# First-layer weighted sums as two float32r matmuls with row sums beside v, in place of weight folding dealt into the first image's attention

## The chip, the core and the metric

The kernel runs on one core of one Trainium2 chip. The core has five engines with a queue each: TensorE (PE, matrix multiplies, with a separate row PEld for the weight loads), VectorE (DVE), ScalarE (ACT), GpSimd (POOL) and SyncE (SP), of which the last only issues DMAs here. Each engine works through its queue in order and waits at an instruction until what it needs is there. The metric is the device time of one execution in microseconds; the number given is the median of three runs.

## The reference

Two attention blocks follow each other on x of shape (8, 512, 32, 32): eight images, 512 channels, T = 1024 positions. The first has eight heads of 64 channels and quantises q, k and v to 8 bits over the whole batch; the second has one head of 512 channels.

```python
# layer 0
h = group_norm(xf, gn_w, gn_b)
qkv = einsum('oc,bct->bot', qkv_w, h) + qkv_b          # then split by head into q, k, v
q, k, v = fake_quant(q), fake_quant(k), fake_quant(v)   # scale from min and max over all images
w = softmax(einsum('bct,bcs->bts', q * scale, k * scale), axis=-1)
a = einsum('bts,bcs->bct', w, v)
x = xf + einsum('oc,bct->bot', proj_w, a) + proj_b
# layer 1
t = group_norm(x)                                       # one head
q, k, v = t @ wq.T + bq, t @ wk.T + bk, t @ wv.T + bv
x = x + (softmax(q @ k.T / sqrt(512)) @ v) @ wp.T + bp
```

Everything is float32. Since the quantisation scales need all images, no score of layer 0 can be computed before q, k and v of all eight images are known.

## The kernel before, in words

Work is cut into tiles of 128 partitions. T is cut into two halves (hf) of 512 and eight blocks (s, t, m) of 128; channels into four blocks (cc, oc, dc) of 128; heads into four pairs (j).

**Phase 1** (lines 213 to 319). For each image, x is loaded and normalised (`norm_steps`, line 99: statistics on VectorE, two tiny matmuls for the group means, then eight writes of h). Eight tiles of q and k (`qkps`, eight matmuls each) and eight tiles of v (`vps`, four each) go through TensorE; VectorE adds the bias, takes max and min, and SP writes the tiles to DRAM. The norm of image b+1 is a generator whose steps are dealt into image b's tiles (line 299). The weight parts of the biases are computed after the first q, k and v tile (`bias`, line 251) by matmuls over all 512 columns. The q, k and v weights are loaded on SP in three column thirds behind the first x (line 240); the second layer's weights go on ScalarE's queue (lines 272 to 274).

**Between.** Lines 323 to 346 reduce the extremes over all partitions and make the scales.

**Phase 2.** `attention` (line 384) runs the first layer's attention as a generator over 512 units (b, j, hf, s), two at a time. `scores` computes one unit's scores for both heads of a pair (`st`, two PSUM buffers of two banks each), ScalarE takes the exp into `pt` (line 405, four buffers), VectorE adds it to a running sum `acc` (lines 408, 410). `weighted` multiplies v by pt for both heads; head 0 writes PSUM partitions 0 to 63 and head 1 partitions 64 to 127 of one bank, so that the two take separate columns of the array. `finish` (line 424) turns `acc` into row sums by two matmuls with ones (`sm`), takes the reciprocal (line 432) and scales (line 434). It is called two units into the next half.

`project` and `layer1` are the work of the second half for one image: `pj` (projection and residual), the second norm, then `g`, `v2ps`, `s2` and `o2`, in chunks of four matmuls that count 4.0 each. The second layer's weights are folded first: wa is a product of wq and wk, wm one of wv and wp (`fold`, line 578).

**The order.** Every matmul made through `mm` (line 92) is tied to the one before it, so TensorE's order is the order of the program text. The loop from line 639 deals attention among the other work: `fold` is interleaved with the first image's attention (`F_FOLD`, line 625), and then for each chunk of image b's other work attention of image b+1 is advanced in proportion (`A_IMAGE / F_IMAGE`). At the steps of the second norm, a negative weight lets attention advance alone by 8, 3 and 3 units of weight (`GN_GAPS`, line 35); the other work then catches up, ahead of its share. On the other engines a scheduler orders instructions by its own estimate.

Of the kernel before, what the change touches and what calls it, by code (L numbers as in the profile page):

```python
# [9 lines left out]
F32 = mybir.dt.float32  # L10
BF = mybir.dt.bfloat16
I32 = mybir.dt.int32
AF = mybir.ActivationFunctionType
# [3 lines left out]
P = 128  # L17
B, C, HH, WW = 8, 512, 32, 32
T = HH * WW
# [27 lines left out]
def attn_pair_kernel(  # L47
# [39 lines left out]
    ident = const.tile([P, P], F32, name="ident")  # L87
    make_identity(nc, ident)

    last_mm = [None]  # L90

    def mm(*args, **kw):
        ins = nc.tensor.matmul(*args, **kw).ins  # L93
        if last_mm[0] is not None:
            tc.add_manual_dep(ins, last_mm[0].name, IN_ORDER, reason="order")
        last_mm[0] = ins


    def norm_steps(src, dst, wcol, bank, nm):
# [32 lines left out]
    def group_norm(src, dst, wcol, bank, nm):  # L132
        for _ in norm_steps(src, dst, wcol, bank, nm):
            pass
# [16 lines left out]
    with ExitStack() as fast:  # L151
# [32 lines left out]
        raw_p = fast.enter_context(tc.tile_pool(name="raw", bufs=3))  # L184
        l1p = fast.enter_context(tc.tile_pool(name="l1p", bufs=1))
        NR0 = B * PAIRS * NH * 2
        chk0 = l1p.tile([NR0, 512], F32, name="chk0")
        chk1 = l1p.tile([B * NH, 512], F32, name="chk1")

        def row_sums(ps, terms):  # L190


            n = len(terms) * CC
            for i, (w, wide) in enumerate(terms):
                for e in range(CC):
                    mm(
                        ps, lhsT=wide[:, e, :], rhs=w[:, e, :],
                        start=(i == 0 and e == 0), stop=(i * CC + e == n - 1),
                    )

        def widen(dst, col):
            for e in range(CC):
                nc.vector.tensor_scalar(
                    dst[:, e, :], ones, vec[:, col + e : col + e + 1], None, ALU.mult
                )

        def by_channel(dst, ps):

            for e in range(CC):
                nc.vector.tensor_mul(ps[:, bass.ts(e, P)], ps[:, bass.ts(e, P)], ident)  # L210
            nc.vector.tensor_reduce(dst, ps.rearrange("p (e n) -> p e n", e=CC), AX.X, ALU.add)

        with tc.tile_pool(name="p1w", bufs=1) as p1w, tc.tile_pool(name="p1", bufs=2) as p1, tc.tile_pool(
# [3 lines left out]

            wn = {}
            for tag, ij in (("h", (NQ1, NK1)), ("v", (NV1, WP1))):
                two = l1p.tile([P, 2, CC, C], F32, tag=tag, name=f"wn_{tag}")  # L220
                for n, i in enumerate(ij):
                    wn[i] = two[:, n]
# [7 lines left out]
            def norm(b):  # L230
                xt = xs.pop(b)
                hs[b] = hn = p1.tile([P, CC, T], F32, tag="h", name=f"h1_{b}")
                return norm_steps(
                    lambda cc, hf: xt[:, cc, bass.ts(hf, 512)],
                    lambda cc, hf: hn[:, cc, bass.ts(hf, 512)],
                    V_GN0W, av_bank, f"a{b}",
                )

            load_x(0)
            for i in range(3):  # L240
                nc.sync.dma_start(
                    wqkv[:, :, bass.ts(i, C)], w_qkv[:, :, bass.ts(i, C)]
                )
            vb = p1w.tile([P, C], F32, name="vb")
            nc.scalar.dma_start(vb, vbias[0:1, :].partition_broadcast(P))
            load_x(1)
            gbb = p1w.tile([P, CC, P], F32, name="gbb")
            widen(gbb, V_GN0B)
            qkb = p1w.tile([P, 2 * PAIRS], F32, name="qkb")

            def bias(i):

                ps = bank(f"bias{i}")
                row_sums(ps, ((wqkv[:, :, bass.ts(i, C)], gbb),))
                if i == 2:
                    nc.vector.tensor_add(vb, vb, ps)  # L256
                    return
                b4 = qkb[:, bass.ts(i, PAIRS)]
                by_channel(b4, ps)
                nc.vector.tensor_add(  # L260
                    b4, b4, vec[:, V_QKB + i * PAIRS : V_QKB + (i + 1) * PAIRS]
                )

            for _ in norm(0):
                pass
            for b in range(B):
                ahead = norm(b + 1) if b + 1 < B else iter(())
                next(ahead, None)
                if b + 2 < B:
                    load_x(b + 2)  # L270
                if b == 1:
                    nc.scalar.dma_start(wp0, w_sq[WP0])
                    for i, w in wn.items():
                        nc.scalar.dma_start(w, w_sq[i])
                hn = hs[b]
                for t in range(2 * PAIRS):
# [3 lines left out]
                    for hf in range(NH):  # L280
                        for cc in range(CC):
                            mm(
# [6 lines left out]
                    if b == 0 and j == 0:  # L289
                        bias(isk)  # L290
# [8 lines left out]
                    if t in (3, 5, 6):  # L299
                        next(ahead, None)  # L300
                for t in range(NT):
                    g = b * NT + t
                    ps = bank(f"vps_{b}_{t}")
                    for cc in range(CC):
                        mm(
# [6 lines left out]
                    if b == 0 and t == 0:  # L312
                        bias(2)
# [5 lines left out]
                del hs[b]  # L319
# [31 lines left out]

        qkp = fast.enter_context(tc.tile_pool(name="qkp", bufs=2))
        ptp = fast.enter_context(tc.tile_pool(name="ptp", bufs=4))
        accp = fast.enter_context(tc.tile_pool(name="accp", bufs=2))
        aop = fast.enter_context(tc.tile_pool(name="aop", bufs=10))
        xp = fast.enter_context(tc.tile_pool(name="xp", bufs=13))
        ptp1 = fast.enter_context(tc.tile_pool(name="ptp1", bufs=10))

# [662 lines left out]
```

## Time and profile before

| | us |
|---|---|
| median of three runs (lowest to highest) | 3114.43 (3112.83 to 3117.67) |
| the profiled execution | 3117.67 |
| its span, first to last instruction | 3115.9 |
| PE busy | 3035.8 |
| VectorE busy | 1688.6 |
| ScalarE busy | 705.0 |
| end of the last v matmul of phase 1 | 703.65 |
| first projection matmul of the first image | 839.35 |
| last projection starts | 2903.86 |

Matmuls of float32 are recorded twice (128x512 f32, x1024 for 512 in the code). Durations of matmuls overlap each other, so the distance between two starts says more than the mean duration. "128*64" in a row of TensorE is the shape of the weights. A row's last part is the idle time of the engine just before the group and what ended it. The mean granted clock was 0.992.

### The profile page before, as it was taken

The numbers are of one execution on the slowest core, as the hardware profiler recorded it, in microseconds if no ns is written. First come the engines' busy times: TensorE is split into PE (matmuls) and PEld (weight loads), VectorE is DVE, ScalarE is ACT, GpSimd is POOL, SyncE is SP. The second block draws the span as 40 slices with busy tenths as digits, with TensorE's granted clock in tenths as the row PEclk, the third lists the DMA queues.
The fourth block names the chain that finished last, engine by engine and source line by source line (L and its number), as shares of the span: only waits on it lengthen the run. The fifth ranks groups of instructions, "written<-read, shape, count | busy, mean of one in ns | idle before, by whom it ended". The sixth has DMA issues, their size and how long they took to land.

```text
span 3115.9 us, 22354 instructions
## 1 busy us (share of the span) xinstructions
PE 3035.8 (97%) x8664; PEld 1162.3 (37%) x8664; DVE 1688.6 (54%) x2024; ACT 705.0 (23%) x793; POOL 20.7 (1%) x28
## 2 busy tenths in 40 slices
PE   6999999999999999999999999999999999999998
PEld 3444444443233333333333333333333333333343
DVE  5555554548955465556455735564555546554322
ACT  0000000005523322333223323232322332233001
POOL 0000000000000000000000000000000000000000
PEclk9999999999999999999999999999999999999999
DMA  5322221113100110101011101100110111000000
GB/s 233 115 102 101 105 104 74 79 77 125 48 21 27 41 48 21 41 28 57 14 59 34 41 20 48 48 21 21 48 48 21 34 34 48 21 21 4 14 10 19
DMA packets 91285, 161.53 MB, mean 52 GB/s; under 512 B 11040, under 2 KB 43808, under 8 KB 90528
## 3 DMA queue, kind: packets, MB, share of 16 engines
q1 hardware_dynamic: 90160, 154.47, 14.2%
q10 hardware_dynamic: 1008, 5.53, 0.4%
q8 instruction: 70, 1.15, 0.2%
q14 instruction: 47, 0.39, 0.0%
HBM read 92.56 MB, written 67.11 MB: 51 GB/s over the span
## 4 chain that ended last, share of the span: by engine, by line
PE 92%; DVE 5%; DMA 1%; issue 1%; ACT 1%; POOL 0%; DVEq 0%; ACTq 0%
PE o L93 15%; PE s L93 15%; PE qkps L93 14%; PE av L93 13%; PE g L93 7%; PE v2ps L93 7%; PE vps L93 7%; PE pj L93 7%; PE st L93 4%; PE sm L93 2%; DVE acc L410 2%; DVE rs L432 2%; DMA wqkv<-in_w_qkv_dram 1%; PE fold L93 1%; PE fold_b L93 0%
## 5 line engine op out<-in xcount | busy, mean ns | idle before, releaser
L405 ACT ACTIVATE pt<-st,esc 128x1024 f32<-128x1024 f32 x512 | 543.1, 1113 | 698.5 <-PE st L93 689.8
L93 PE MATMUL av<-pt,v 128*64 128x512 f32 x2048 | 507.8, 617 | 0.0
L410 DVE TENSOR_TENSOR acc<-acc,pt 128x1024 f32<-128x1024 f32 x384 | 467.1, 1217 | 56.5 <-ACT pt L405 44.0
L93 PE MATMUL o<-p,v 128*128 128x512 f32 x1024 | 466.5, 602 | 3.0 <-ACT rs L564 1.4
L93 PE MATMUL s<-g,h 128*128 128x512 f32 x1024 | 465.2, 601 | 0.0
L93 PE MATMUL qkps<-h,wqkv 128*128 128x512 f32 x1024 | 447.4, 597 | 8.0 <-DMA wqkv<-in_w_qkv_dram 8.0
L93 PEld LDWEIGHTS o<-p,v 128*128 128x128 f32 x1024 | 186.3, 190 | 276.4 <-issue 233.3
L93 PEld LDWEIGHTS s<-g,h 128*128 128x128 f32 x1024 | 187.0, 190 | 269.8 <-issue 230.0
L93 PEld LDWEIGHTS qkps<-h,wqkv 128*128 128x128 f32 x1024 | 194.4, 191 | 247.9 <-issue 246.0
L432 DVE RECIPROCAL rs<-rs 128x512 f32<-128x512 f32 x64 | 214.5, 3351 | 82.0 <-ACT rs L431 81.7
L93 PE MATMUL g<-h,wa 128*128 128x512 f32 x512 | 233.1, 607 | 4.6 <-DVE h L126 4.6
L93 PE MATMUL pj<-ao,wp 128*128 128x512 f32 x512 | 233.0, 602 | 4.1 <-ACT rs L431 4.1
L93 PEld LDWEIGHTS av<-pt,v 128*64 128x64 f32 x2048 | 126.2, 138 | 269.1 <-issue 266.2
L93 PE MATMUL v2ps<-wm,h 128*128 128x512 f32 x512 | 222.9, 594 | 0.0
L93 PE MATMUL vps<-wqkv,h 128*128 128x512 f32 x512 | 221.3, 592 | 0.8 <-DVE vb L256 0.8
L293 DVE TENSOR_SCALAR_CACHE_REDUCE qk<-qkps,qkb 128x1024 f32<-128x1024 f32 x64 | 82.2, 1284 | 217.0 <-PE qkps L93 217.0
L529 DVE COPY v<-v2ps 128x512 f32<-128x512 f32 x64 | 44.2, 691 | 252.7 <-PE v2ps L93 252.7
L541 ACT ACTIVATE p<-s 128x512 f32<-128x512 f32 x128 | 76.5, 598 | 433.6 <-PE s L93 433.6
L545 DVE TENSOR_TENSOR acc<-acc,p 128x512 f32<-128x512 f32 x96 | 66.3, 691 | 196.2 <-ACT p L541 196.2
L93 PE MATMUL st<-q,k 64*128 64x512 bf16 x1024 | 159.0, 386 | 4.9 <-ACT pt L405 4.9
L589 ACT COPY wa<-fold 128x512 f32<-128x512 f32 x4 | 2.3, 586 | 702.0 <-PE fold L93 702.0
L93 PEld LDWEIGHTS g<-h,wa 128*128 128x128 f32 x512 | 95.9, 193 | 142.3 <-issue 111.5
(114 smaller groups left out, 1521.9 us busy)
## 6 DMA issues: line engine op xcount, KB each, us to landing
x<-in_x_dram SPq DMA_DIRECT2D x32, 512.0 KB, 5.7
q_d<-qk SPq DMA_DIRECT2D x32, 512.0 KB, 2.6
raw<-q_d SPq DMA_DIRECT2D x32, 512.0 KB, 3.4
k_d<-qk SPq DMA_DIRECT2D x32, 512.0 KB, 2.6
raw<-k_d SPq DMA_DIRECT2D x32, 512.0 KB, 4.2
v_d<-v SPq DMA_DIRECT2D x64, 256.0 KB, 2.0
raw<-v_d SPq DMA_DIRECT2D x32, 512.0 KB, 4.3
x<-in_x_dram SPq DMA_DIRECT2D x64, 256.0 KB, 2.6
```

The source lines that it names most:

```text
L93: ins = nc.tensor.matmul(*args, **kw).ins
L293: nc.vector.tensor_scalar(qk, ps.rearrange("p a n -> p (a n)"), qkb[:, t : t + 1], None, ALU.add, ALU.max, accum_out=mx[:, g : g + 1],)
L405: nc.scalar.activation(pt, st, AF.Exp, scale=esc)
L410: nc.vector.tensor_add(accs[b, j, hf], accs[b, j, hf], pt)
L432: nc.vector.reciprocal(rs, rs)
L529: nc.vector.tensor_copy(vt[:, t, :], ps)
L541: nc.scalar.activation(pt, ps, AF.Exp, scale=SM1)
L545: nc.vector.tensor_add(acc, acc, pt)
L589: nc.scalar.copy(dst[:, e, :], ps)
```

## The change

Two parts of the kernel are replaced.

1. *Weighted sums.* For each unit, ScalarE computes the exp twice: once into `hi`, of type float32r (a float32 with fewer bits of mantissa[...]), and once in place in PSUM. VectorE subtracts hi from it into `lo`, also float32r. Each head then has a PSUM bank of its own, and `weighted` makes four float32r matmuls with 128 columns: head 0's weights are its 64 columns of v and then 64 columns of ones, head 1's are ones and then v. The other half of each bank so holds the row sums, and `finish` copies both halves out on ScalarE, takes the reciprocal and scales. The running sums `acc` and the `sm` matmuls of the first layer go. hi and lo have three buffers each. `finish` is called right after the last weighted sum of a half.
2. *Weights and order.* The folding is done between phase 1 and attention, nothing is dealt into the first image's attention, and the bias sums are matmuls of one column. The norm of image b+1 is written whole ahead of image b's tiles, and those matmuls are no longer tied in order. The q, k and v weights are loaded on ScalarE's queue by channel block. The check of the row sums moves behind all other work.

```diff
-            row_sums(ps, ((wqkv[:, :, bass.ts(i, C)], gbb),))
+            norm(0)
+            for t in range(2 * PAIRS):
+                for cc in range(CC):
+                    nc.tensor.matmul(
+                        ps[:, t : t + 1], lhsT=wqkv[:, cc, bass.ts(t, P)],
+                        rhs=vec[:, V_GN0B + cc : V_GN0B + cc + 1],
+                        start=(cc == 0), stop=(cc == CC - 1),
+                    )
...
             for b in range(B):
-                ahead = norm(b + 1) if b + 1 < B else iter(())
-                next(ahead, None)
+                if b + 1 < B:
+                    norm(b + 1)
...
-            for i in range(3):
-                nc.sync.dma_start(
-                    wqkv[:, :, bass.ts(i, C)], w_qkv[:, :, bass.ts(i, C)]
-                )
+            for cc in range(CC):
+                nc.scalar.dma_start(wqkv[:, cc, :], w_qkv[:, cc, :])
...
+            for dst, lw, rw in ((wa, NQ1, NK1), (wm, NV1, WP1)):
+                for e in range(CC):
+                    ps = bank(f"fold_{lw}_{e}")
+                    for d in range(CC):
+                        nc.tensor.matmul(
+                            ps, lhsT=wn[lw][:, d, bass.ts(e, P)], rhs=wn[rw][:, d, :],
+                            start=(d == 0), stop=(d == CC - 1),
+                        )
+                    nc.scalar.copy(dst[:, e, :], ps)
...
-        ptp = fast.enter_context(tc.tile_pool(name="ptp", bufs=4))
+        ptp = fast.enter_context(tc.tile_pool(name="ptp", bufs=3))
+        vts = [l1p.tile([P, NT, 3, CH], F32R, name=f"v_{i}") for i in range(2)]
+        for vt in vts:
+            for t in range(NT):
+                nc.scalar.copy(vt[:, t, 1, :], ones[:, 0:CH])
...
-                pt = ptp.tile([P, 2, 512], F32, tag="p", name=f"pt_{nm}_{s}")
-                nc.scalar.activation(pt, st, AF.Exp, scale=esc)
-                if s == 1:
-                    accs[b, j, hf] = accp.tile([P, 2, 512], F32, tag="acc", name=f"acc_{nm}")
-                    nc.vector.tensor_add(accs[b, j, hf], pts[u - 1], pt)
-                elif s > 1:
-                    nc.vector.tensor_add(accs[b, j, hf], accs[b, j, hf], pt)
+                hi = ptp.tile([P, 2, 512], F32R, tag="hi", name=f"hi_{nm}")
+                nc.scalar.activation(hi, st, AF.Exp, scale=esc)
+                nc.scalar.activation(st, st, AF.Exp, scale=esc)
+                lo = ptp.tile([P, 2, 512], F32R, tag="lo", name=f"lo_{nm}")
+                nc.vector.tensor_sub(lo, st, hi)
...
-                for i, r in enumerate(HALF):
-                    mm(
-                        avs[b, j, hf][r, :], lhsT=pairs[b, j][2][:, s, r], rhs=pt[:, i, :],
-                        start=(s == 0), stop=(s == NT - 1),
-                    )
+                for i, bk in enumerate(avs[b, j, hf]):
+                    w = pairs[b, j][2][:, s, i : i + 2, :].rearrange("p i d -> p (i d)")
+                    for n, part in enumerate(parts):
+                        mm(
+                            bk, lhsT=w, rhs=part[:, i, :],
+                            start=(s == 0 and n == 0), stop=(s == NT - 1 and n == 1),
+                        )
...
-                sm = bank(f"sm_{nm}")
-                for i, r in enumerate(HALF):
-                    mm(sm[r, :], lhsT=ones[:, 0:CH], rhs=acc[:, i, :], start=True, stop=True)
-                nc.scalar.copy(rs, sm)
+                for i, bk in enumerate(avs.pop((b, j, hf))):
+                    nc.scalar.copy(rs[HALF[i], :], bk[HALF[1 - i], :])
+                    nc.scalar.copy(aot[HALF[i], :], bk[HALF[i], :])
                 nc.vector.reciprocal(rs, rs)
...
-                if s == 2 and u >= NT:
-                    finish(*units[u - NT][:3])
-                    yield 1.0, b
+                if s == NT - 2:
+                    finish(b, j, hf)
...
-        A_IMAGE = PAIRS * NH * (NT * 1.5 + 1.0)
+        A_IMAGE = PAIRS * NH * NT * 1.25
...
-        folded = 0.0
-        for w in fold():
-            folded += w
-            while pos < (folded - F_FIRST) * A_IMAGE / F_FOLD:
-                advance()
```

## The prediction

> **What bounds the kernel now.** I began with the page's busy times and its chain, then read the groups by shape, and last the timeline of TensorE around the first image's attention and around one second-layer norm.
>
> ```profile
> PE 3035.8 (97%) x8664; PEld 1162.3 (37%) x8664; DVE 1688.6 (54%) x2024; ACT 705.0 (23%) x793; POOL 20.7 (1%) x28
> ...
> PE 92%; DVE 5%; DMA 1%; issue 1%; ACT 1%; POOL 0%; DVEq 0%; ACTq 0%
> ```
>
> TensorE (PE) is busy for 97% and is 92% of the chain; VectorE and ScalarE are followers. The groups:
>
> ```profile
> L405 ACT ACTIVATE pt<-st,esc 128x1024 f32<-128x1024 f32 x512 | 543.1, 1113 | 698.5 <-PE st L93 689.8
> L93 PE MATMUL av<-pt,v 128*64 128x512 f32 x2048 | 507.8, 617 | 0.0
> L93 PE MATMUL st<-q,k 64*128 64x512 bf16 x1024 | 159.0, 386 | 4.9 <-ACT pt L405 4.9
> L432 DVE RECIPROCAL rs<-rs 128x512 f32<-128x512 f32 x64 | 214.5, 3351 | 82.0 <-ACT rs L431 81.7
> L93 PE MATMUL sm<-acc,ones 128*64 128x512 f32 x256 | 69.3, 620 | 0.1
> ```
>
> An f32 matmul leaves two records. The two heads of a pair have 64 columns each and share the array, so av has 2048 records. Durations overlap, so prices come from the distance of starts. The chain's row "676.35 27.48 PE vps L93 x64" gives 429.3 ns a record, 858.6 ns an f32 matmul. The timeline of TensorE, from the end of one projection to the folded-key matmuls (columns: start, us):
>
> ```profile
> 1176.14 0.61 PE L93 MATMUL st<-q,k 64*128 64x512 bf16 x4
> 1176.67 1.94 PE L93 MATMUL av<-pt,v 128*64 128x512 f32 x8
> 1178.54 0.61 PE L93 MATMUL st<-q,k 64*128 64x512 bf16 x4
> ...
> 1193.29 0.58 PE L93 MATMUL gps_b<-gd_b,gavg 128*128 128x4 f32 x2 [3.73 <-DVE gd_b L116]
> ...
> 1198.08 7.13 PE L93 MATMUL g<-h,wa 128*128 128x512 f32 x16 [0.42 <-DVE h L126]
> ```
>
> Two units of attention cost 0.54 us of scores and 1.87 us of weighted sums. Between chunks of other work lies this norm gap of 22 us, filled with attention alone. The same view shows that first-image attention with the folding takes 703.65 to 839.35 (135.7 us); each of seven mixed images takes 294.8 (g at 1198.08 and 1492.85); the last stretch, from 2903.86, takes 212.
>
> **What the Trainium skill says.** "FP8 and Floating Point Precision", TensorE Precision Notes: true FP32 is four passes, reduced precision one. The trace agrees on four: 858.6/4 = 214.7 ns, and the bf16 scores fit one pass a row (0.54 us for two overlapped pairs). No row here is float32r. "TensorE: Matmul & The Clock Gate", LDWEIGHTS: columns/1.2, so 107 ns for 128; the trace has 190 ns per f32 record, hidden under 429. "TensorEngine Tiling (Array Packing)", Key Properties: changing the tiling mode drains; the trace agrees, since scores plus weighted sums are 2.15 us of passes and take 2.41. "ScalarE: Activation LUTs", What ACT_TABLE_LOAD costs: back-to-back ACTIVATEs overlap by 93 ns. Here four exps take 4.14 us, 1.01 each.
>
> **The change, part by part.**
>
> *Weighted sums.* Before, four passes, both heads at once: 4 x 214.7 = 0.86 us a unit. After, two heads x two parts, each on the whole array: again 4 x 214.7 = 0.86. So "one-pass" saves no passes; it saves at most the exposed switching, 1.87 - 1.72 = 0.15 us per two units. The real gain is the row-sum matmul: 64 x about 1.02 us = 65 us.
>
> *ScalarE and VectorE.* Each unit now needs two exps (2.02 us) and a subtraction from PSUM. A 128x1024 TENSOR_TENSOR takes 1.22 (the acc rows); PSUM as a source is no dearer at 512 elements (0.690 in v<-vps against 0.691 in acc<-acc,p). The second exp writes PSUM in place, which no row shows; the skill's ScalarE page calls PSUM the faster destination, so 1.01 is taken as the upper end, and rival (d) is the lower. The subtraction replaces the acc add, so VectorE gains little work. But acc gated nobody; now the score bank is free only after both exps and the subtraction, and there are two banks. Score buffers also hold hi and lo, three of each (before: four pt). In the changed program's order TensorE has scores(u+2), scores(u+3), weighted(u), weighted(u+1); hi(u+3) needs the buffer that weighted(u) frees. Attention alone, after the exps of u+1 end: subtraction 1.3 with its wait, scores 0.3, weighted(u) 0.86, wait 0.2: hi(u+3) starts at 2.66, not 2.02. Two units take 2.02 + 2.66 = 4.68 us, against 2.41 before. Behind hi(u+3) ScalarE queues every later exp and TensorE the next scores.
>
> *Finish.* Four 64x512 copies replace one (0.59 us each, 0.5 pitched: 2.05). They and the reciprocal (3.35) stand ahead of the third subtraction of the next half: 5.4 us instead of 2.0, so +3.4 per eight units. Among chunks this is hidden by 9 us of TensorE work per cycle.
>
> *First image.* Four cycles of 4.68, 3.4, and 0.5 for quantisation make 22.6 us per eight units; x 8 plus 3 to fill = 184.
>
> *Folding moved ahead.* 32 matmuls x 0.86 = 27.5 us. The 64 bias matmuls of one column cost two weight loads each; the tiny gps pair costs 0.31 (1185.76 to 1186.07), two exposed loads 0.38. I take 23 us (20 to 26). Beside it run only its eight evacuations and the sixteen copies of ones on ScalarE, the 13 loads of x for the second layer that now stand ahead of q, k and v on SP (3.4 MB, some 8 us), those three loads (7.8 us on the chain before) and six quantisations (4.5): about 21 us, so 50 us of folding cover them; without it the first scores would come 21 us after the last v. So pj starts at 703.65 + 27.5 + 23 + 184 = 938, not 839.35: +99 us.
>
> *Start.* wqkv moves to ScalarE's queue ahead of the second-layer weights, x alone stays on SP. Before, TensorE waited for wqkv to 26.78 and did 10.8 us of bias matmuls later. After, the 3 MB of wqkv share with as much x at the 400 GB/s of the first slices: from 4 us, landed near 19. Then 29 bias columns x 0.38 (11), the last vb matmul (0.9) and the rest of the norm (3.3) come before the first scores: about 34. Net 34 - 26.8 - 10.8 = -3 us (-8 to +8). The second image's norm now stands whole ahead of its matmuls in TensorE's order; its statistics are done a whole image (83 us) earlier, so only the one matmul for the variance waits, under 1 us an image.
>
> *A mixed image.* Outside the gap: 294.8 - 22 = 272.8. Take out 26 pairs of units x 2.41 and six row sums (62.7 + 6.1); put in 25 pairs x 2.26 (56.5; the gap now holds seven): 260.5. The six cycles with one chunk last only 5.9 us, as long as the exps of two units, a start of 0.5 and a subtraction (4.04 + 0.5 + 1.3): +0.5 each, +3. Six have a chunk ahead of weighted, which delays hi(u+3) to 5.0 us; exps and subtraction then end at 8.4 of a 9.2 us cycle, and other exps of 0.60 can push them over: +0.5 each, +3. Fewer mode changes: -3. The gap: VectorE has 13 subtractions, six quantisations, a reciprocal and the norm between the last pj and g, in order; taking for each step the later of 2.02 and its VectorE work gives 34, the three buffers add 5: 39. Sum 302.5 (+-8), against 294.8: +7.7, x 7 = +54.
>
> *End.* The check of sums moves behind the last output: four 0.68 us operations and an all-reduce, +3.
>
> Sum against the profiled span 3115.9: +99 + 54 - 3 + 3 = 3269; I take 3277 for one or two more slips of in-order VectorE per image. That execution took 3117.67, 1.8 over its span, and 3.2 over the median of 3114.43; so 3275 for the median.
>
> **The rivals.** (a) One-pass weights are not hidden: 107 to 190 ns must fit under 214.7 instead of 429. For: the f32 loads show 190. Against: 190 is below 214.7. At 0.1 us exposed per matmul, 0.8 per two units: 175 pairs, 140 us, and 30 in the gaps and the first image: 3445.
>
> (b) Half pace, since float32r still reads four bytes: 429 ns, +1.72 per two units: 175 x 1.72 = 300, plus 60 where attention is alone: 3636. Against: the f32 passes of 214.7 ns read four bytes too. If it is no one-pass at all, four passes: over 4000.
>
> (c) Buffers hide better (ScalarE at 2.02 throughout, gap 30): first image 160, images 296: about 3200, or down to 3150.
>
> (d) Not slower: the second exp, PSUM to PSUM, is cheap, so attention alone stays bound by TensorE. The place is the first image (64 units) and seven gaps (91 units); at TensorE's pace these would be 104 and 119 us shorter: 3054. It decides when the mean pace there falls from about 2.6 to 1.53 us a unit, a second exp of 0.5 us. Against: exps of 512 and 1024 elements take 598 and 1113 ns, so only 83 ns is fixed and another destination can't save half a microsecond.
>
> **How the numbers follow.** Main case 0.72 (3210 to 3330), (a) 0.10, (b) 0.06, (c) 0.06, (d) 0.04, and 0.02 for a time equal to before (about 0.2% is what a measurement can tell from no change). The range from 3170 to 3420 holds the main case, half of (c) and the lighter half of (a). Faster 0.04, same 0.02, slower 0.94.
>
> **What would show it.** Right: matmuls of av at 215 ns starts; no sm rows of 64 columns; ScalarE near 1250 us busy, saturated between 755 and 935; TensorE waiting there and in the norm gaps for the subtraction or the exps; pj first near 935; images near 303 us. Wrong: av starts at 300 ns or more; weighted sums waiting among chunks in every cycle (VectorE's order); or TensorE busy through the first attention.

## The result and the profile after

The changed kernel takes 3248.93 us (median of four runs, 3243.33 to 3254.29) against 3115.26 us for the kernel before in runs beside it (3112.83 to 3117.67). The ratio is 1.0429, with a 95% interval of 1.0408 to 1.0450: slower. The forecast was 3275, in a range from 3170 to 3420, with 0.94 on slower.

The profiled execution has a span of 3249.2 us, against 3115.9. The 133.3 us between them lie in three places. "First projection" is the first `pj` of the first image; an image is the distance of two starts of `g`.

| us | before | predicted | after |
|---|---|---|---|
| first projection | 839.35 | 935 | 943.6 |
| one of seven mixed images | 294.9 | 302.5 | 298.9 |
| of it, the gap at the second norm | 22 | 39 | 39.5 |
| first to last projection | 2064.5 | 2118 | 2094.9 |
| after the last projection starts | 212 | 215 | 210.7 |

So 104.3 us come before the first projection, 30.4 from the seven mixed images, and 1.3 are gained at the end.

From the page of the changed kernel, the busy times, the row of the clock that TensorE was granted in 40 slices, and the chain by engine:

```profile
PE 3060.5 (94%) x8552; PEld 1490.4 (46%) x8552; DVE 1765.1 (54%) x2056; ACT 1333.6 (41%) x1513; POOL 18.1 (1%) x26
...
PEclk9999999996788999999899989998999999999999
...
PE 88%; ACT 4%; DVE 3%; issue 3%; DMA 1%; POOL 0%; ACTq 0%; DVEq 0%
```

TensorE's busy time hardly grew (3060.5 against 3035.8), but the span grew by 133. In the chain ScalarE's share rose from 1% to 4% and that of issue from 1% to 3%, while VectorE's fell from 5% to 3% and TensorE's from 92% to 88%. And the clock row has a dent, in the slices of the first image's attention. The groups that answer to those shown of before:

```profile
L415 DVE TENSOR_TENSOR lo<-st,hi 128x1024 fp32r<-128x1024 f32 x512 | 623.8, 1219 | 456.0 <-ACT st L413 452.6
L412 ACT ACTIVATE hi<-st,esc 128x1024 fp32r<-128x1024 f32 x512 | 571.4, 1116 | 632.4 <-PE av L352 324.5 <-PE st L352 305.5
L413 ACT ACTIVATE st<-st,esc 128x1024 f32<-128x1024 f32 x512 | 556.5, 1087 | 0.0
L352 PE MATMUL av<-hi,v 128*128 128x512 f32 x1024 | 485.9, 475 | 0.4
L352 PE MATMUL st<-q,k 64*128 64x512 bf16 x1024 | 180.6, 403 | 162.7 <-DVE lo L415 155.2
```

ScalarE waits 324.5 us for weighted sums and 305.5 for scores before it may write `hi` (part of it no loss, since among other work attention has to wait for its turn), and TensorE waits 155.2 us for the subtraction before it may write the next scores. The chain of waits in the middle of the first image's attention (start, length, work on the path) shows the waits for weighted sums and for the subtraction as one closed loop:

```profile
821.14 1.11 ACT hi L412
822.26 0.99 ACT st L413
...
823.27 1.24 DVE lo L415
...
824.55 0.39 PE st L352 x2
824.94 0.90 PE av L352 x3
...
825.93 1.12 ACT hi L412
...
829.72 1.56 PE av L352 x3
...
831.36 0.09 ACT hi L412
```

Two exps of one unit, then the subtraction that frees the score bank, then the next scores, then three of the four matmuls of one unit's weighted sums, of which the third reads a `hi` buffer for the last time and so releases ScalarE: 4.79 us from 821.14 to 825.93, for two units. Nothing in it overlaps anything else in it. The next round takes 5.43 us: the three matmuls take 1.56 us there instead of 0.90, with a granted clock of 0.60 from 829.33 to 831.28 against 1.00 from 824.55 to 825.84.

### The profile page after: what moved, and what is told of

Its sections match the earlier page's. It is cut to its first block, busy times and chain, and to the rows that moved or that the text cites. A ratio compares the mean times of both kernels' runs of the same rounds, so it can differ in the third digit from the quotient of the medians.

```text
span 3249.2 us, 23183 instructions
## 1 busy us (share of the span) xinstructions
PE 3060.5 (94%) x8552; PEld 1490.4 (46%) x8552; DVE 1765.1 (54%) x2056; ACT 1333.6 (41%) x1513; POOL 18.1 (1%) x26
## 4 chain that ended last, share of the span: by engine, by line
PE 88%; ACT 4%; DVE 3%; issue 3%; DMA 1%; POOL 0%; ACTq 0%; DVEq 0%
PE qkps L244 14%; PE o L352 14%; PE s L352 14%; PE av L352 13%; PE g L352 7%; PE pj L352 7%; PE v2ps L352 7%; PE vps L263 7%; PE st L352 4%; DVE lo L415 2%; ACT st L413 2%; ACT hi L412 1%; PE fold L281 1%; PE fold_b L295 1%; PE sm L352 0%
## 5 line engine op out<-in xcount | busy, mean ns | idle before, releaser
L415 DVE TENSOR_TENSOR lo<-st,hi 128x1024 fp32r<-128x1024 f32 x512 | 623.8, 1219 | 456.0 <-ACT st L413 452.6
L412 ACT ACTIVATE hi<-st,esc 128x1024 fp32r<-128x1024 f32 x512 | 571.4, 1116 | 632.4 <-PE av L352 324.5
L413 ACT ACTIVATE st<-st,esc 128x1024 f32<-128x1024 f32 x512 | 556.5, 1087 | 0.0
L352 PE MATMUL av<-hi,v 128*128 128x512 f32 x1024 | 485.9, 475 | 0.4
L352 PE MATMUL o<-p,v 128*128 128x512 f32 x1024 | 455.9, 594 | 1.4 <-ACT rs L563 1.4
L352 PE MATMUL av<-lo,v 128*128 128x512 f32 x1024 | 438.9, 429 | 0.0
L352 PE MATMUL st<-q,k 64*128 64x512 bf16 x1024 | 180.6, 403 | 162.7 <-DVE lo L415 155.2
L352 PEld LDWEIGHTS av<-hi,v 128*128 128x128 f32 x1024 | 213.0, 208 | 128.7 <-issue 77.6
L352 PEld LDWEIGHTS av<-lo,v 128*128 128x128 f32 x1024 | 215.4, 210 | 52.5 <-issue 13.4
L352 PEld LDWEIGHTS <-k 64*128 64x128 bf16 x1024 | 38.9, 95 | 359.8 <-issue 303.0
## 6 DMA issues: line engine op xcount, KB each, us to landing
v_d<-v SPq DMA_DIRECT2D x64, 256.0 KB, 2.0
x<-in_x_dram SPq DMA_DIRECT2D x64, 256.0 KB, 2.7
```

Source lines behind the costliest of these rows:

```text
L412: nc.scalar.activation(hi, st, AF.Exp, scale=esc)
L413: nc.scalar.activation(st, st, AF.Exp, scale=esc)
L415: nc.vector.tensor_sub(lo, st, hi)
```

## The experiments

Each kernel was timed against the kernel before on the same chip (3113 to 3116 us in all groups). The table is for the comparisons; "ahead" is from the end of the last v matmul of phase 1 to the first projection, with the folding in it.

| kernel | time, us | ratio (95%) | ahead, us | an image, us |
|---|---|---|---|---|
| before | 3114 | 1 | 135.7 | 294.9 |
| changed | 3248.93 | 1.0429 (1.0408 to 1.0450) | 242.7 | 298.9 |
| weighted sums alone | 3226.97 | 1.0359 (1.0338 to 1.0380) | 217 | 298.7 |
| order and folding alone | 3142.87 | 1.0084 (1.0067 to 1.0101) | 170 | 294.3 |
| changed, four `hi` buffers | 3219.44 | 1.0334 (1.0317 to 1.0351) | 227 | 296.1 |
| changed, second exp to SBUF | 3151.97 | 1.0120 (1.0103 to 1.0137) | 212 | 289.0 |
| both of these | 3144.37 | 1.0096 (1.0080 to 1.0113) | 210 | 288.4 |
| weighted sums alone, second exp to SBUF | 3126.23 | 1.0040 (1.0025 to 1.0054) | 186 | 289.5 |
| changed, `hi` alone | 2863.92 | 0.9193 (0.9178 to 0.9208) | 159 | 256.0 |
| old order, `hi` alone | 2842.06 | 0.9126 (0.9111 to 0.9141) | 135 | 256.0 |
| mixed: old form in the first image only | 3087.49 | 0.9911 (0.9894 to 0.9927) | 144 | 289.0 |
| mixed, old form in the gaps too | 3091.17 | 0.9924 (0.9907 to 0.9940) | 142 | 289.8 |

### Which half of the change costs what

The kernel before with only its attention replaced, the old order and the dealt folding kept:

```diff
-                pt = ptp.tile([P, 2, 512], F32, tag="p", name=f"pt_{nm}_{s}")
-                nc.scalar.activation(pt, st, AF.Exp, scale=esc)
...
+                nc.scalar.activation(hi, st, AF.Exp, scale=esc)
+                nc.scalar.activation(st, st, AF.Exp, scale=esc)
+                lo = ptp.tile([P, 2, 512], F32R, tag="lo", name=f"lo_{nm}")
+                nc.vector.tensor_sub(lo, st, hi)
...
```

> The kernel before with only the weighted sums changed (two exps, subtraction, four float32r matmuls, row sums beside v); folding stays dealt into the first image's attention, first phase as before. Theory A (attention alone is paced by exps, subtraction and buffers, and folding fits into its waits): first image about 188 us from the last v to the first projection, images 299, sum 704 + 188 + 7 x 299 + 212 = 3197 us (3180 to 3215). Theory C (the order of folding and the first phase is what cost the time): 3115 to 3145 us.

And the changed kernel with the attention of before, so that only the order, the bias sums and the folding are new:

```diff
-                hi = ptp.tile([P, 2, 512], F32R, tag="hi", name=f"hi_{nm}")
-                nc.scalar.activation(hi, st, AF.Exp, scale=esc)
...
+                pt = ptp.tile([P, 2, 512], F32, tag="p", name=f"pt_{nm}_{s}")
+                nc.scalar.activation(pt, st, AF.Exp, scale=esc)
...
```

> The changed kernel with the attention of before (one exp, four-pass weighted sums of both heads at once, row-sum matmuls); only the folding ahead of attention, the bias columns and the first phase's order are changed. Theory A: last v at 701 us, 59 us of folding and quantisation, attention alone some 90 us (64 x 1.2, eight row sums, a few waits), images 295, end 212: 3127 us (3118 to 3140). Theory C: 3180 us or more.

Measured by span, the weighted sums alone add 110.7 us and the order alone 28.3; together they add 133.3. So the halves nearly add up, and the weighted sums are four fifths of the loss. Both expectations were too hopeful. In the first run the first image took 206.7 us from its first scores: some 31 of the 41 us of folding (48 matmuls of 0.859 us) are dealt into it, and it is 23 us longer than the same attention without folding (183.2). The folding matmuls stand in TensorE's order inside the loop shown above and lengthen it; only about a quarter of them fell into time in which TensorE would have waited anyway.

In the second run the first image took 110.4 us, more than expected. The stretch by engine (columns: from and to, length, busy TensorE, weight loads, VectorE, ScalarE, GpSimd, then the granted clock, the share of the DMA engines and GB/s) in that run:

```profile
760.80:871.20 110.40, 94.40 (x416) 23.93 (x416) 108.83 (x98) 75.08 (x73) 0.00 (x0) 0.93 0.24 77
```

VectorE is busy for 108.83 of 110.40 us. With the folding taken out, the old attention is bound by VectorE (running sums, reciprocals, quantisation), not by TensorE. In the kernel before, the same stretch with 31 us of folding in it takes 125.4 us, 15 more: half of the dealt folding was hidden, and the change gave this cover up. That is some 16 of the 34 us by which "ahead" grows in this run. Of the rest, 6.94 are a wait of TensorE after the folding, taken up below, and some 11 the bias sums of the folding: as matmuls of one column they take 25.2 us, where sixteen matmuls of 512 columns at 0.859 us, 13.7 us, stood before.

### The buffer and the score bank

In the loop two links can be cut. The first run gives `hi` a fourth buffer (the residual's tiles go from 13 to 11 to make room):

```diff
-                hi = ptp.tile([P, 2, 512], F32R, tag="hi", name=f"hi_{nm}")
+                hi = ptp.tile([P, 2, 512], F32R, tag="hi", bufs=4, name=f"hi_{nm}")
```

> The changed kernel with four buffers of hi instead of three (the pool of x for the second half has 11 tiles instead of 13 to make room). Theory A, hi buffer: the first exp of unit u+3 waits for the weighted sums of unit u; with a fourth buffer this wait (324 us of ScalarE's idle time) goes, the first image's attention falls from 183 to about 162 us and each norm gap from 39.5 to about 35: 3195 us (3180 to 3215). Theory B, score banks: the loop through two score banks alone (scores, two exps, subtraction) sets the pace and ScalarE only waits elsewhere: 3235 us or more.

3219.44 lies between the two theories: about 30 us less, 169.4 us for the first image against 183.2, and 296.1 for an image against 298.9. The waits of this run (who waited for whom: us in total, times, longest):

```profile
ACT hi L412 <- PE st L352: 376.3, 132, 29.9
DVE lo L415 <- ACT st L413: 361.2, 269, 6.2
...
PE st L352 <- DVE lo L415: 143.9, 112, 5.0
```

ScalarE's wait for `av` no longer appears among its waits (324.5 us in the changed kernel), but its wait for the scores has grown from 305.5 to 376.3 us, and the scores wait for the subtraction nearly as before (143.9 against 155.2). The second run cuts the other link. The second exp goes to an SBUF tile of two buffers, so that the score bank is free after the two exps and not after VectorE (residual's tiles 9):

```diff
-                nc.scalar.activation(st, st, AF.Exp, scale=esc)
+                ex = ptp.tile([P, 2, 512], F32, tag="ex", bufs=2, name=f"ex_{nm}")
+                nc.scalar.activation(ex, st, AF.Exp, scale=esc)
...
-                nc.vector.tensor_sub(lo, st, hi)
+                nc.vector.tensor_sub(lo, ex, hi)
```

> The changed kernel with the second exp written to an SBUF tile of two buffers instead of in place to PSUM, so that the score bank is free after the two exps and not after VectorE's subtraction; hi and lo keep three buffers. Theory S (the scores of u+2 wait for the subtraction, and this is the larger half of what attention alone loses): first image 183 -> 160 to 165 us, the gap at the second norm 39.5 -> 33 to 35, an image 299 -> 292 to 295; whole time 3185 (3170 to 3205). Theory B (the three hi buffers decide, since hi(u+3) waits for weighted(u) however early the scores are there): first image 178 or more, whole time 3230 to 3250.

This takes 97 us off, more than expected: the first image takes 152.9 us, an image 289.0, and the gap at the second norm 30.6. The subtraction itself is no faster from SBUF (1219 ns in both kernels), so its source does not explain the gain. The chain of waits in the same place of this run:

```profile
823.60 1.11 ACT hi L412
824.71 1.00 ACT ex L414
825.72 1.01 ACT hi L412
826.72 1.00 ACT ex L414
827.73 1.01 ACT hi L412
```

ScalarE runs exp after exp without a wait, 4.02 us for two units (twice the 2.01 from 825.72 to 827.73) instead of 4.79, and that is the whole path there. Its stretch reads (columns as before):

```profile
760.70:913.60 152.90, 104.84 (x389) 58.61 (x390) 125.68 (x111) 148.94 (x159) 0.00 (x0) 0.89 0.18 59
```

ScalarE is busy for 148.94 of 152.90 us. The granted clock is higher too (0.89 against 0.75). If the buffer were a second wait of its own, a fourth one should now help again:

```diff
-                hi = ptp.tile([P, 2, 512], F32R, tag="hi", name=f"hi_{nm}")
+                hi = ptp.tile([P, 2, 512], F32R, tag="hi", bufs=4, name=f"hi_{nm}")
```

> The changed order with the second exp in SBUF and, besides, hi with four buffers (the residual's tiles 8, layer 1's exp tiles 9, to make room). If buffer and score bank are two waits in a row, each with its own gain: another 25 to 30 us off, 3120 (3112 to 3128). If the buffer only mattered because the score bank came back late, or because ScalarE's two exps a unit now set the pace: 3143 to 3155, the same as with three.

3144.37 and 3151.97 have overlapping intervals; the first image takes 152.5 us against 152.9. The fourth buffer is worth 30 us while the bank is held and next to nothing once it is free. So the held bank is the larger link, and the buffer counts only along with it: scores that come late make weighted sums that come late, and these free the buffer.

The same cut in the kernel with the old order (against the kernel with the weighted sums alone; residual's tiles 9 here too):

```diff
-                nc.scalar.activation(st, st, AF.Exp, scale=esc)
+                ex = ptp.tile([P, 2, 512], F32, tag="ex", bufs=2, name=f"ex_{nm}")
+                nc.scalar.activation(ex, st, AF.Exp, scale=esc)
...
-                nc.vector.tensor_sub(lo, st, hi)
+                nc.vector.tensor_sub(lo, ex, hi)
```

> The order and folding of the kernel before with the new weighted sums, and the second exp written to SBUF (two buffers). If the score bank is what made the dealt folding come out exposed: last v to first projection 217 -> 185 to 195 us, images 298.7 -> 292 to 295, whole time 3165 (3150 to 3180), still slower than before by 1 to 2%. If the three hi buffers or ScalarE's two exps a unit decide: 3205 to 3230.

3126.23, 101 us less than with the bank held, and 0.4% above the kernel before. This is well below the expected range: its stretch ahead of the first projection came out as expected (186), but each of its images gained more (289.5).

### What the lower part costs

The changed kernel without `lo`: no second exp, no subtraction, two matmuls instead of four. The exp then keeps only float32r's bits, so this computes less than the reference asks for:

```diff
-                nc.scalar.activation(st, st, AF.Exp, scale=esc)
-                lo = ptp.tile([P, 2, 512], F32R, tag="lo", name=f"lo_{nm}")
-                nc.vector.tensor_sub(lo, st, hi)
-                pts[u] = hi, lo
+                pts[u] = (hi,)
...
```

> The changed kernel without lo: the second exp, the subtraction and the two matmuls of lo are left out, so the exp keeps only float32r's bits. Theory A: attention alone is then bound by one exp a unit plus the copies of each half (about 90 us for the first image, gap about 22 us), and a pair of units costs TensorE about 0.93 us less among chunks: images about 258 us; 701 + 59 + 90 + 7 x 258 + 210 = 2866 us (2830 to 2910). If one-pass matmuls were the cost (their weight loads not hidden and TensorE short of time), the image would fall only to about 275: 2990 us or more.

2863.92, as expected. The same in the old order (against the kernel with the weighted sums alone):

```diff
-                nc.scalar.activation(st, st, AF.Exp, scale=esc)
-                lo = ptp.tile([P, 2, 512], F32R, tag="lo", name=f"lo_{nm}")
-                nc.vector.tensor_sub(lo, st, hi)
-                pts[u] = hi, lo
+                pts[u] = (hi,)
...
```

> The order and folding of the kernel before (folding dealt into the first image's attention) with weighted sums of hi alone: no second exp, no subtraction, no lo part, so the exp keeps only float32r's bits. If dealing the folding hides it when attention alone is bound by ScalarE at one exp a unit and TensorE is half free: last v to first projection 158.9 (this arithmetic in the changed order: 700.9 to 859.8) -> 125 to 140 us, whole time 2835 (2815 to 2850). If the dealt folding only lengthens each cycle of scores, exp and weighted sums, as it did with both parts: 2855 to 2880, no better than the changed order.

2842.06, inside the expected range. The lower part therefore costs 385 us in either order, and without it the one-pass form is worth 8.7% over the kernel before. Four pairs of kernels now differ in order, bias sums and folding alone, with four forms of attention: the new order costs 28 us (old form), 22 (both parts), 26 (second exp to SBUF) and 22 (`hi` alone). This part of the change was a loss of its own, whatever stands beside it.

### The clock

In the first image's attention of the changed kernel the mean clock is 0.75, and weighted sums of 1.7 us stand beside others of 0.9. To see whether the clock is a cause or a follower, eight matmuls of 128x512 in bf16, which nobody reads, were put beside every two units of the first image:

```diff
...
+                    for _ in range(2 if units[u][0] == 0 else 0):
+                        mm(bank_w[0], lhsT=pairs[b, j][1][:, 0:P], rhs=pairs[b, j][0][:, 0:512], start=True, stop=True)
                     scores(u + 2)
...
+                    for _ in range(6 if units[u][0] == 0 else 0):
+                        mm(bank_w[0], lhsT=pairs[b, j][1][:, 0:P], rhs=pairs[b, j][0][:, 0:512], start=True, stop=True)
                     scores(u + 3)
```

> The changed kernel with eight more bf16 matmuls of 128x512 per two units of the first image's attention, into a bank of their own, which nobody reads (two ahead of the scores of u+2, six ahead of the scores of u+3). They keep TensorE active through the stretch in which the trace of the changed kernel shows a mean clock of 0.75. Theory H (the half clock lengthens the wait of ScalarE's hi(u+3), because weighted(u) then takes 1.7 us instead of 0.9): clock near 1.0 there, the first image's attention 183 -> 165 to 172 us, whole time 3230 to 3238. Theory I (ScalarE, the score banks and the in-order chain set the pace and the clock is only a consequence of the waiting): 180 to 190 us there, 3246 to 3260.

The stretch in the changed kernel, and then in this one:

```profile
760.40:943.60 183.20, 121.75 (x389) 69.97 (x390) 128.47 (x112) 152.32 (x160) 0.00 (x0) 0.75 0.16 49
```

```profile
757.40:933.00 175.60, 153.72 (x645) 75.30 (x646) 126.04 (x110) 151.04 (x159) 0.00 (x0) 0.97 0.14 46
```

The clock went from 0.75 to 0.97 and the stretch from 183.2 to 175.6 us, between the two theories. From a first exp to the one eight units later, after the first eight, 22.2 us on the mean became 21.15. The whole time, 3243.40 (ratio 1.0423, 1.0406 to 1.0441), can't be told from the changed kernel's. The added matmuls take TensorE's time too, so 7.6 us is what the clock gave back net of them; against the 30 us of the freed bank in the same stretch it is the smaller part.

### Where the folding was not covered

After the last folding matmul TensorE stands for 6.84 us. The changed kernel's chain there, and one line of the waits of the DMA queue on SP:

```profile
701.08 27.47 PE fold L281 x64
728.55 25.01 PE fold_b L295 x128
753.57 3.69 DMA raw<-q_d
```

```profile
SPq L376 <- PE fold_b L295: 43.7, 1, 43.7
```

The first loads of q, k and v go out only when the folding ends. The changed kernel opens the pool of these raw tiles after the pools of phase 1 are closed; the kernel before opened it ahead of them. The run opens it ahead again:

```diff
+        raw_p = fast.enter_context(tc.tile_pool(name="raw", bufs=3))
         with tc.tile_pool(name="p1w", bufs=1) as p1w, tc.tile_pool(name="p1", bufs=2) as p1, tc.tile_pool(
...
-        raw_p = fast.enter_context(tc.tile_pool(name="raw", bufs=3))
```

> The changed kernel with the pool of the raw q, k and v tiles opened ahead of phase 1, as in the kernel before, instead of after the pools that hold the folding's weights are closed. If the loads waited for the room of these weights (SP's wait of 43.7 us for the last folding matmul), the first three raw loads go out near 710 us, behind the thirteen x loads, and not at 753.6; TensorE's wait between the last folding matmul and the first scores falls from 6.8 to 3 to 4 us, because the quantisations still stand behind the bias sum of the folding in VectorE's order or write to room freed then; the whole time falls by 3 to 4 us, which one run can't show. If the loads waited for something else: they still go out within 1 us of the folding's end, and the wait stays at 6.5 to 7.5 us.

The loads of q, k and v of the first pair now start at 55.6, 77.2 and 124.3 us, much earlier still than expected, since they need only the first image's tiles. TensorE's timeline at the end of the folding, changed kernel and then this run:

```profile
752.76 0.78 PE L295 MATMUL fold_b<-vec,wn 128*128 128x1 f32 x3
760.38 1.04 PE L352 MATMUL st<-q,k 64*128 64x512 bf16 x4 [6.84 <-issue]
```

```profile
748.87 1.84 PE L296 MATMUL fold_b<-vec,wn 128*128 128x1 f32 x8
752.34 1.04 PE L352 MATMUL st<-q,k 64*128 64x512 bf16 x4 [1.63 <-issue]
```

The wait falls from 6.84 to 1.63 us, further than expected; in the seven runs with the changed order and the late pool it is 6.8 to 6.95 us. So the loads had waited for the room that the folding's weights held. One run of 3247.26 us can't show 5 us in the whole: the first projection comes 10.4 us earlier in it, but the stretch to the last one is 7.1 longer, and why stays open. In the kernel before, the first of these loads went out at 49.6 us.

### Putting the new form where it pays

If the loss sits where attention is alone, the old form belongs there and the new one elsewhere. In the old order, with the second exp to SBUF, the first image keeps the f32 exp, the running sum and the four-pass matmuls:

```diff
+                if b == 0:
+                    nc.scalar.activation(pt, st, AF.Exp, scale=esc)
+                    if s == 1:
+                        accs[b, j, hf] = ptp.tile([P, 2, 512], F32, tag="ex", bufs=2, name=f"acc_{nm}")
+                        nc.vector.tensor_add(accs[b, j, hf], pts[u - 1], pt)
+                    elif s > 1:
+                        nc.vector.tensor_add(accs[b, j, hf], accs[b, j, hf], pt)
+                    pts[u] = pt
+                    return
                 hi = ptp.tile([P, 2, 512], F32R, tag="hi", name=f"hi_{nm}")
```

> The dealt order with the second exp in SBUF, but the first image's attention in the form of the kernel before (f32 exp once, running sum on VectorE, four-pass weighted sums with both heads side by side); images 1 to 7 in the new form. Theory S (what remains of the loss sits where attention is alone, above all in the first image: 186 us there against 135.7 in the kernel before, while an image among other work takes 289 against 294.8): last v to first projection 134 to 142 us, images 289 to 290, whole time 3076 (3065 to 3095), faster than the kernel before by 0.6 to 1.6%. If the new form is not worth more than the old one among other work, or the two forms disturb each other: 3105 or more.

3087.49, a ratio of 0.9911 (0.9894 to 0.9927): 0.9% faster than the kernel before, with every part of the computation kept. By the marks of its trace the first projection comes at 847.0 (7.6 later than before), the stretch to the last one is 35.7 us shorter, the end 1.6. The first stretch was 2 us longer than the expected range; why was not looked into.

Another run did the same in the gaps at the second norm, with the second half of pair 0 and the first half of pair 1 in the old form:

```diff
-                if b == 0:
+                if b == 0 or (j, hf) in ((0, 1), (1, 0)):
```

> As the mixed kernel, and in images 1 to 7 also the two halves of 64 that fall into the gap at the second norm (second half of pair 0, first half of pair 1) in the form of the kernel before. If the gap is longer only because attention alone is bound by ScalarE and VectorE in the new form: gap 33.5 -> 22 to 25 us, the chunks beside it 3 us dearer, images 289 -> 281 to 284, whole time 3025 (3010 to 3050). If the gap is set by VectorE's norm work and quantisation, or a switch of form costs as much as it saves: 3065 or more.

3091.17, no gain, so the rival holds. The chain of waits in one gap of this run, from where TensorE waits for the norm's matmul at 1203.48 to `g`:

```profile
1197.13 1.17 DVE acc L422
...
1200.08 0.08 DVE gmean_b L112
...
1200.19 1.23 DVE acc L422
1201.41 0.07 DVE gd_b L115
...
1202.22 1.14 DVE acc L422
1203.36 0.09 DVE gd_b L117
...
1203.48 0.61 PE gps_b L94 x2
...
1205.60 3.74 DVE h L127 x8
1209.35 1.14 DVE lo L430
...
1210.51 1.12 ACT ex L428
...
1211.68 0.39 PE st L94 x2
1212.07 3.20 PE g L94 x7
```

The old form's running sums, 1.14 to 1.23 us each, stand between the norm's steps of under 0.1 us on VectorE, whose queue carries one operation of about 1.2 us a unit in either form. This gap takes 30.1 us, from the end of the last `pj` at 1181.95 to `g`, against 22 in the kernel before, and the record shows where the 8 us lie. To the norm's second matmul it takes 21.5 us instead of 17.2; it holds seven pairs of units instead of six. From there to the first write of `h` it takes 2.1 instead of 4.2. From that write to `g` it takes 6.4 instead of 0.6: all eight writes of `h` stand ahead of the subtraction of the first unit in the new form, the next unit's second exp starts only when this subtraction is done, the next scores wait for that exp, and `g` stands behind these scores in TensorE's order. On the mean of seven gaps the mixed kernel without this edit takes some 24 us for the first step and 3.7 for the last, this one 22 and 6.4. So the switch back to the new form takes again what the old form saved: both halves of the rival are at work.

## Why the prediction was right

**The loop in attention alone** was named in the prediction with its parts: the bank held until the subtraction, weighted(u) ahead of hi(u+3), three buffers. It was priced at 4.68 us per two units and measures 4.79 where its matmuls run at full clock. The first image was put at 184 us and took 183.2, but that this is so close is luck. Eight units were to take 22.6 us and take 22.2 on the mean, after the first eight. In the run with the added matmuls, at a clock of 0.97, they take 21.15: four rounds of 4.79 and 2.0 for the boundary of a half, which was put at 3.4 and 0.5. What was too dear there is in good part made up by 1.0 us of lower clock, which the prediction did not have. The rival that put ScalarE at 2.02 us a unit throughout, with 160 for the first image and 30 for the gap, is just what appears once the score bank is freed (152.9 and 30.6). What the prediction did not see is which of the two links decides: it told them as one sum, and the runs give the bank 97 us and the buffer 30 only while the bank is held. And "acc gated nobody" does not hold where attention is alone. There VectorE is busy for 108.83 of 110.40 us in the run with the order alone, which is 3.45 us per two units and not the 2.41 that the prediction named; in the gap of the kernel before it is busy for 21.41 of 21.94 us.

**The second exp in place** was taken at 1.01 us a start. The group has 1087 ns against 1116 for the first exp, which goes to SBUF, and in the run with both to SBUF they start 1.01 us apart. The page of the Trainium skill, "ScalarE: Activation LUTs", "Step-by-step: what each stage is for", says that ScalarE reaches PSUM faster than SBUF; the trace has 29 ns of it in the records, at the price of a bank held for 1.24 us more. The rival of a cheap second exp (0.5 us) falls.

**Weighted sums in one pass, weight loads hidden.** The traces of before have no float32r matmul, so one pass was an assumption. The starts are 0.23 us apart at full clock, where 214.7 ns was expected and 300 ns was named as the sign of error. The loads take 208 to 210 ns in the records. So the rival of exposed loads and that of half pace both fall, and eight starts of 0.23 are 1.84 us per two units against 1.87 before: the matmuls themselves save next to nothing, as the prediction had it. Of the 13.4 us that an image gains outside the gap, some 7 are row sums (seven, where the prediction counted six), and 2.4 are one pair of units that the longer gap takes over. The remaining 4 are as much as the prediction's 0.15 us per two units for exposed switching, but where they lie was not traced, and its further 3 us for fewer mode changes do not appear.

**A mixed image** was 3.6 us too dear. The gap is right (39 against 39.5). Outside it 263.5 was predicted and 259.4 measured, and there TensorE is busy without a break:

```profile
1028.50:1287.90 259.40, 259.40 (x754) 124.68 (x753) 143.69 (x140) 134.27 (x153) 0.00 (x0) 0.99 0.10 35
```

The step that failed is "+0.5 each, +3" and "+0.5 each, +3", for cycles that were said to overrun, and the 8 us for slips of VectorE's order: none of it shows in that stretch. Without the 6 us the sum outside the gap would have been 257.5, 1.9 below the measured. By span, from the 3277 that the forecast took: 23.6 less from the images, 8 less for the slips, 4.3 less at the end, and 8.3 more at the first projection, which is 3249.4.

**The folding.** "50 us of folding cover" the loads and the quantisation: wrong. The matmuls took 27.47 and 25.01 (27.5 and 23 were predicted), but the loads had to wait for their room, and TensorE stood for 6.84 us. The prediction took the loads as ready beside the folding without asking where their tiles lie; the pool's move was in the program and not counted. The 34 us that the order alone adds to "ahead" were in the sum only as part of a difference of two whole stretches; the lost cover of the first image, some 16 of them, the prediction did not name.

**Start and end.** The last v matmul ends 2.7 us earlier (3 predicted). The end is 1.3 us shorter, where the check of sums was to add 3; why stays open.

## What to carry to other kernels

When a second reader is added to a PSUM bank, price the bank's time until the last reader lets go, and follow what the in-order producer has queued behind its next write: here an in-place exp that saved 29 ns in its record held the bank for a subtraction, and that cost 97 us in all. A form that takes work off TensorE pays where TensorE is the bound (in the mixed kernel some 14 us an image outside the gap) and loses where attention stands alone (8 us in each gap); choose it by stretch, not for the whole kernel, and look for what else shares the queue that becomes the bound and for what a switch of form costs. A pool that is opened later than before can delay a first load by the whole life of the tiles whose room it takes.

## What the runs showed of the hardware

- Float32r matmuls of 128x512 start 0.23 us apart at full clock (granted 1.00 from 847.60 to 849.00) and 0.43 at half (0.50 from 844.80 to 846.50), where one of the four passes of an f32 matmul works out to 0.215. The timeline of TensorE in the first attention of the changed kernel, around one wait:

```profile
844.82 0.63 PE L352 MATMUL av<-hi,v 128*128 128x512 f32 x1
845.25 0.63 PE L352 MATMUL av<-lo,v 128*128 128x512 f32 x1
...
847.25 0.39 PE L352 MATMUL st<-q,k 64*128 64x512 bf16 x2 [0.83 <-DVE lo L415]
...
847.90 0.39 PE L352 MATMUL av<-lo,v 128*128 128x512 f32 x1
848.13 0.40 PE L352 MATMUL av<-hi,v 128*128 128x512 f32 x1
```

- The pace switches between rounds of one loop, though after the first rounds, which have a wait of 5.74 us, no wait of TensorE in the first image's attention is longer than 2.4 us. "TensorE: Matmul & The Clock Gate", "A second HAM failure mode: psum-queue depth-cycling", in the Trainium skill tells of a clock that swings between half and full where TensorE idles briefly and often between groups; this trace agrees, with a mean of 0.75 at 66% busy (121.75 of 183.20 us) and 0.78 in the gap.
- A one-column f32 matmul cost 0.35 to 0.39 us (64 of them in 22.3 to 25.1 us in the runs), almost half of one of 512 columns (0.86). Two weight loads stand beside each. Part of the price is the clock: TensorE is busy without a break there, and yet the trace of the changed kernel has a clock of 0.50 for it (columns as before):

```profile
739.00:753.50 14.50, 14.50 (x69) 14.46 (x68) 0.16 (x1) 0.00 (x0) 0.00 (x0) 0.50 0.00 0
```

  At that clock one such matmul takes 0.42 us (69 records in 14.50 us, two for each). In the run with the pool opened early the first of them, at a clock of 0.90, take 0.25 us (57 records in 7.20 us).
